# All eight experts over half of the tokens at a time in the first sequence, in tiles of two unit chunks

## The chip, the cores and the metric

The kernel runs on one core of one Trainium2 chip. The core has five engines with an instruction stream each: TensorE (PE in the profile, its weight loads as PEld), VectorE (DVE), ScalarE (ACT), GpSimd (POOL) and SyncE (SP), whose queue issues the kernel's DMAs. Every engine takes its own instructions in order and waits on semaphores for the others. The metric is the device time of one execution in microseconds. Before the change it was 1373.06 us, the median of three runs (1371.94 to 1373.44).

## What is computed

Eight independent sequences of 512 tokens with 128 features go through four layers, each with a layer norm ahead of it and a residual sum behind: a selective scan ("mamba"), a mixture of eight experts, a windowed attention with 16 heads, and the same mixture of experts again. All is float32. The mixture of experts is where most products are:

```python
router_probs = softmax(x @ w_router)             # (tokens, 8)
gate_weights = softmax(x @ w_gating / 0.1)
g = einsum('bsh,ehf->ebsf', x, w_gate)           # 8 experts, 128 -> 512 units
u = einsum('bsh,ehf->ebsf', x, w_up)
h = silu(g) * u
expert_out = einsum('ebsf,efh->ebsh', h, w_down) # 512 units -> 128
cw = router_probs * gate_weights
cw = cw / (sum(cw, axis=-1, keepdims=True) + 1e-09)
out = einsum('ebsh,bse->bsh', expert_out, cw)
```

Every token goes through all eight experts.

## The kernel before, in words

**The experts.** Tokens lie on the free axis (up to 512 of them, one bank of PSUM), features or units on the 128 partitions. The 512 units of an expert are four chunks of 128 (`NFC`). For each chunk TensorE makes g and u, and a little later adds the chunk's part to y, the expert's output. Each of these is three matmuls (`matmul3`), since every float32 operand is held as the sum of two rounded parts, "hi" and "lo": hi x hi, lo x hi, hi x lo.

Between u and y lies what this text calls the h pipeline (`hidden`, lines 1180 to 1212): ScalarE takes silu of g from the bank, VectorE multiplies it with u, ScalarE or VectorE rounds h to its hi part ("CAST h<-h"), and POOL (or VectorE) subtracts to get lo. While ScalarE holds the tables of an exponential set early in the kernel, silu is made in a second form: tanh on ScalarE and one VectorE instruction more (`halved`). When the four chunks of y are there, VectorE multiplies y with the expert's weights for the tokens, which SP has spread over the partitions from a small tensor in DRAM (`cwb`, lines 1138 to 1155), and POOL adds it to `acc` (`weighted`, lines 1114 to 1136). For the first expert VectorE writes `acc` itself.

**The stream.** All of this is one stream over two mixture layers (k), eight sequences (b), the passes of a sequence (`passes`, lines 1106 to 1112) and the four chunks. For all sequences but the very first a pass is one expert over all 512 tokens. In the first sequence the experts 0 to 3 (`SPLIT = 4`) go over the first 256 tokens, then over the second 256, and then experts 4 to 7 over all 512:

```python
parts = [(e, slice(c * HALF, c * HALF + HALF)) for c in range(2) for e in range(SPLIT)]
return parts + [(e, whole) for e in range(SPLIT, NE)]
```

The scan of sequence 0 is itself made in two halves of tokens, so its first half goes into the experts before its second half is done.

**The order.** A planner written in Python (`Clock`, `Lanes`) decides at build time in which order instructions stand on each engine. The stream of g, u and y is its main line on TensorE; beside it run "lanes" that it puts in where their inputs are due by its own cost figures: the h pipelines, the scans of the following sequences, the layer norms and routing (`ffn_prep`), the attention, and at the start the loading of the expert weights (`ffn_weights`). The eight banks are shared out by it: experts may hold six (`MOST`), a new y a seventh; the others may hold four. A tile of g or u takes one bank, whatever its width, from its first product until ScalarE (g) or VectorE (u) has read it.

**The weights.** The 24 weight matrices of 256 KB are loaded once by SP into a few stage tiles. ScalarE rounds each to hi ("CAST wu<-stageu") and POOL or VectorE subtracts to get lo; then its stage tile is free for the load three places on. Those of the experts from 5 on (`EARLY`) are rounded only after the first half of sequence 0 has been prepared.

**The scan of a following sequence** (`mamba_front`, `mamba_back`) needs on ScalarE two silus, two tanhs, then after a table load an exponential and a logarithm over `mdelta` and four exponentials `mdec`; on TensorE the transposition tp_m, the product mh, the products mde and mbc, eight spreads (mbx and mcc, one 512-wide product each) and the output product mo; on VectorE the convolution, four scans and a dozen products. Its result goes to DRAM (`x_1`), is loaded again (`x_f`), normed, and transposed (tp_f) into the next sequence's `xt_f`.

Since operations are recorded by one helper, nearly all instructions show its line, L264, and are told apart by their tiles.

Of the kernel before, what the change touches and what calls it, by code (L numbers as in the profile page):

```python
# [108 lines left out]
PREP_DUE = 0.8  # L109
ATT_LEAD = 2.5  # L110
EARLY = 5
SPLIT = 4
EARLIEST = 2 * (DEPTH + 1)


# [257 lines left out]
def block_kernel(ctx: ExitStack, tc: tile.TileContext, x, pack_a, pack_b, pack_c, w_qkv, mask, mask_t, w_o,  # L373
# [110 lines left out]
    def matmul3(dst, w, v, start=True, stop=True, after=0.0):  # L484

        clock.beside = False
        pe.matmul(dst, w[0], v[0], start=start, stop=False, after=after)
        pe.matmul(dst, w[1], v[0], start=False, stop=False)
        return pe.matmul(dst, w[0], v[1], start=False, stop=stop)
# [609 lines left out]
    def ffn_stream():  # L1099

        pending = []
        spread = []
        state = {}
        ends = {}

        def passes(k, b):

            whole = slice(0, L)
            if k or b:
                return [(e, whole) for e in range(NE)]  # L1110
            parts = [(e, slice(c * HALF, c * HALF + HALF)) for c in range(2) for e in range(SPLIT)]
            return parts + [(e, whole) for e in range(SPLIT, NE)]

        def weighted(k, b, e, cs, y, there):

            key = k, b, e, cs.start
            if ("cwb", key) not in state:
                yield lambda: ("cwb", key) in state
            cwb, come = state.pop(("cwb", key))
            yield "V", max(there, come)  # L1120
            left = state.setdefault(("left", k, b), [len(passes(k, b))])
            if e == 0:
# [12 lines left out]
            if left[0] == 0:  # L1135
                lanes.add(ffn_finish(k, b, state.pop(("acc", k, b))), rank=FRANK, ready=t)

        def spreads():

            for k in range(2):  # L1140
                for b in range(B):
                    todo = passes(k, b)
                    for i, (e, cs) in enumerate(todo):
                        at = k * B + b + (i * NFC + NFC - 1) / (len(todo) * NFC)
                        yield lambda: ("cw", k, b) in done and done["cw", k, b][2] >= cs.stop
                        yield lambda: pos[0] >= at and len(spread) < 2
                        cwd, there, _ = done["cw", k, b]
                        yield "S", there
                        spread.append(e)
                        n = cs.stop - cs.start  # L1150
                        cwb = fp.tile([P, L], F32, tag="cwb", name=f"cwb{k}_{b}_{e}_{cs.start}", bufs=2)[:, :n]
                        state["cwb", (k, b, e, cs.start)] = cwb, sp.dma_start(
                            out=cwb.rearrange("p (t q) -> p t q", q=P),
                            in_=cwd[None, cs.start // P : cs.stop // P, e, :].to_broadcast([P, n // P, P]),
                        )

        def can(f, hs, sure=0.0):

            return len(hs) > 2 and clock.there(hs[2] + sure) and (f > 0 or bank("experts", MOST + 1))

        def downs():

            while len(pending) > SHALLOW:
                f, hs = pending[0][4:]
                if len(pending) < DEPTH and not can(f, hs, SURE):
                    break
                while not can(f, hs):
                    yield True
                down(*pending.pop(0))

        def down(k, b, e, cs, f, hs):
            if f == 0:
                state["y"], = take("experts", [[P, L]], [f"y{k}_{b}_{e}"])
            y = state["y"][:, : cs.stop - cs.start]
            w = [t[:, f * P : (f + 1) * P] for t in wgt["d", e]]
            t = matmul3(y, w, hs, start=(f == 0), stop=(f == NFC - 1))
            if f == NFC - 1:
                lanes.hurry(weighted(k, b, e, cs, y, t))

        def hidden(i, g, there, us, hs, nm):  # L1180

            if i > 2:
                yield lambda: ends.pop(("lo", i - 3), None)
            yield "A", there
            n = size(g)
            h = fp.tile([P, L], F32, tag="h", name=f"h{nm}", bufs=3)[:, :n]

            halved = clock.table == 0 and clock.now < clock.hold
            if halved:
                act.activation(h, g, AF.Tanh, scale=0.5)  # L1190
                yield "V"
                s = dve.scalar_tensor_tensor(h, h, 1.0, g, ALU.add, ALU.mult)
            else:
                s = act.activation(h, g, AF.Silu)
# [12 lines left out]
            (dve.tensor_copy if v + HI_BIAS < a else act.copy)(hs[0], h)  # L1207
            yield "PV"
            ends["lo", i] = quicker(n, V_BIAS).tensor_tensor(hs[1], h, hs[0].bitcast(F32), ALU.subtract)
            hs.append(ends["lo", i])  # L1210

        lanes.hurry(spreads())
        i = 0
        for k in range(2):
            for b in range(B):
                todo = passes(k, b)
                for n, (e, cs) in enumerate(todo):
                    while (k, b) not in ready or ready[k, b][1] < cs.stop:
                        yield True
                    xt = [t[:, cs] for t in ready[k, b][0]]  # L1220
                    if n == len(todo) - 1:
                        ready.pop((k, b))
                    while ("d", e) not in done:
                        yield True
                    for f in range(NFC):
                        nm = f"{k}_{b}_{e}_{cs.start}_{f}"
                        fs = slice(f * P, (f + 1) * P)
                        pos[0] = k * B + b + (n * NFC + f) / (len(todo) * NFC)
                        while not bank("experts", MOST):
                            yield True  # L1230
                        g = take("experts", [[P, L]], [f"g{nm}"])[0][:, : cs.stop - cs.start]
                        t = matmul3(g, [t[:, fs] for t in wgt["g", e]], xt)
                        us = []
                        hs = [
                            fp.tile([P, L], F32R, tag=f"h{j}", name=f"h{j}{nm}", bufs=DEPTH + 1)[:, : size(g)]
                            for j in range(2)
                        ]
                        lanes.hurry(hidden(i, g, t, us, hs, nm))
                        yield
                        while not bank("experts", MOST):  # L1240
                            yield True
                        u = take("experts", [[P, L]], [f"u{nm}"])[0][:, : size(g)]
                        us += u, matmul3(u, [t[:, fs] for t in wgt["u", e]], xt)
                        yield
                        yield from downs()
                        pending.append((k, b, e, cs, f, hs))
                        i += 1
                        yield
        while pending:
# [528 lines left out]
```

## Time and profile before

| | before |
|---|---|
| median of three runs | 1373.06 us |
| the profiled execution's own time | 1372.12 us |
| its span, first to last instruction | 1370.3 us |
| mean granted TensorE clock | 0.994 |
| TensorE busy | 1334.7 us, 97% |
| VectorE busy | 1040.2 us, 76% |
| ScalarE busy | 966.5 us, 71% |
| POOL busy | 931.4 us, 68% |
| TensorE's first g of sequence 0 | at 41.12 us |
| first 512-wide g (expert 4) | at 106.53 us |
| the output product mo of sequence 1's scan | at 99.72 us |

Times in the trace count from the first instruction. A row of the order of time has the start, the length, the engine, the line, the operation with its output and inputs, the shape and the number of equal instructions. The ends of matmuls are modelled, so the distance between the starts of rows that follow each other is a better measure of what a matmul costs than its length. A row of waits has the waiting engine and tile, the releasing engine and tile, the sum in us, the number of waits and the longest. A row of stages has the stage, its length, for each engine its busy time and (x) instructions, then the clock granted to TensorE as a share of full speed, the share of DMA and GB/s.

### The profile page before, as it was taken

What the parts mean: (1) busy time and instruction counts of PE and PEld (TensorE: products, weight loads), DVE (VectorE), ACT (ScalarE), POOL (GpSimd) and SP (SyncE); (2) the same over time, 40 slices, a digit from 0 to 9 for tenths busy, and PEclk for the clock granted to TensorE, in tenths of its full rate; (3) what the DMA queues carried; (4) which work ended last, traced back from release to release, by engine and by line L of the source; (5) the groups of instructions that cost most, each with busy time, mean ns of one, the idle gap of its engine ahead of it and who ended that gap; (6) DMA issues with size and microseconds to landing.
All of it is one profiled execution on the core that took longest, in us unless ns stands there. A gap on an engine that the chain in (4) does not pass through costs nothing. (4 is left out here: it accounts for less than half of the span.)

```text
span 1370.3 us, 29702 instructions
## 1 busy us (share of the span) xinstructions
PE 1334.7 (97%) x10328; PEld 1053.5 (77%) x10328; DVE 1040.2 (76%) x3132; ACT 966.5 (71%) x1701; POOL 931.4 (68%) x1050
## 2 busy tenths in 40 slices
PE   7789999999999999999999999999999999999997
PEld 6667777777878877777777777777777777778886
DVE  6886888788888556898878887888878878754443
ACT  7478587786785556776777787877777768775654
POOL 4576676666767577676766757767576676677776
PEclk9999999999999999999999999999999999999999
DMA  3221222233221431335435455453454443232111
GB/s 125 74 68 50 64 46 75 65 86 86 54 60 35 70 77 46 77 71 121 98 88 111 87 117 111 93 107 86 106 116 90 113 91 74 65 71 54 40 39 39
DMA packets 230846, 107.77 MB, mean 79 GB/s; under 512 B 86401, under 2 KB 226600, under 8 KB 230696
## 3 DMA queue, kind: packets, MB, share of 16 engines
q1 hardware_dynamic: 230696, 105.87, 34.2%
q8 instruction: 82, 1.34, 0.4%
q14 instruction: 68, 0.56, 0.1%
HBM read 77.64 MB, written 27.79 MB: 77 GB/s over the span
## 5 line engine op out<-in xcount | busy, mean ns | idle before, releaser
L264 POOL TENSOR_TENSOR h<-h,h 128x512 fp32r<-128x512 f32 (+1 forms) x508 | 641.9, 1272 | 299.4 <-ACT h L264 236.3
L264 PE MATMUL u<-xt_f,wu 128*128 128x512 f32 (+1 forms) x1584 | 454.7, 395 | 7.5 <-ACT h L264 6.1
L264 PE MATMUL g<-xt_f,wg 128*128 128x512 f32 (+1 forms) x1584 | 452.5, 394 | 3.4 <-DVE cwb L264 1.0
L264 PE MATMUL y<-h,wd 128*128 128x512 f32 (+1 forms) x1584 | 449.9, 393 | 5.0 <-POOL h L264 2.8
L264 ACT CAST h<-h 128x512 fp32r<-128x512 f32 (+1 forms) x467 | 279.5, 604 | 200.4 <-DVE h L264 198.7
L264 DVE TENSOR_TENSOR h<-u,h 128x512 f32<-128x512 f32 (+1 forms) x424 | 283.0, 673 | 168.9 <-PE u L264 104.4
L264 ACT ACTIVATE h<-g 128x512 f32<-128x512 f32 (+1 forms) x528 | 305.0, 583 | 113.9 <-PE g L264 85.6
L264 PEld LDWEIGHTS u<-xt_f,wu 128*128 128x128 f32 x1584 | 288.4, 189 | 78.1 <-ACT h L264 9.8
L264 PEld LDWEIGHTS y<-h,wd 128*128 128x128 f32 x1584 | 289.9, 188 | 75.2 <-POOL h L264 3.9
L264 PEld LDWEIGHTS g<-xt_f,wg 128*128 128x128 f32 x1584 | 289.7, 189 | 72.8 <-DVE cwb L264 2.1
L264 POOL TENSOR_TENSOR acc<-acc,cwb 128x512 f32<-128x512 f32 (+1 forms) x115 | 146.7, 1275 | 52.4 <-DVE cwb L264 31.3
L264 ACT ACT_TABLE_LOAD x110 | 141.1, 1283 | 26.0 <-PE g L264 24.3
L264 DVE CUSTOM_DVE_ANT_0 amasked<-as,maskq 128x60 f32<-128x60 f32 x640 | 95.3, 213 | 4.0 <-PE as L264 3.5
L264 DVE TENSOR_TENSOR cwb<-y,cwb 128x512 f32<-128x512 f32 (+1 forms) x115 | 77.2, 671 | 19.2 <-PE y L264 10.8
L264 DVE TENSOR_TENSOR apt<-aw,maskk 125x400 f32<-125x400 f32 (+2 forms) x160 | 87.0, 572 | 0.1
L264 DVE SCALAR_TENSOR_TENSOR h<-h,g 128x512 f32<-128x512 f32 (+1 forms) x104 | 67.2, 649 | 23.4 <-ACT h L264 22.4
L264 ACT ACTIVATE apt<-apt 125x400 f32<-125x400 f32 (+2 forms) x160 | 81.8, 541 | 0.4
L264 DVE SCALAR_TENSOR_TENSOR h<-u,h 128x512 f32<-128x512 f32 (+1 forms) x104 | 67.6, 652 | 3.1
L264 DVE DVE_READ_ACCUMULATOR2_ANT amx<- 128x1 f32 x640 | 52.2, 82 | 0.0
L264 PEld LDWEIGHTS ao<-apt,v 125*32 125x32 f32 (+2 forms) x1280 | 27.4, 110 | 14.6 <-issue 4.7
L264 DVE CAST h<-h 128x512 fp32r<-128x512 f32 (+1 forms) x61 | 37.8, 624 | 1.0
L264 DVE COPY v<-avr 125x128 f32<-125x128 f32 (+2 forms) x40 | 21.1, 529 | 21.7 <-PE ao L264 18.0
(195 smaller groups left out, 1232.0 us busy)
## 6 DMA issues: line engine op xcount, KB each, us to landing
cwb<-cwd_f SPq DMA_DIRECT2D x124, 256.0 KB
aqd<-apc SPq DMA_DIRECT2D x32, 192.0 KB
ks<-aqd SPq DMA_DIRECT2D x48, 93.8 KB
x_fo<-x SPq DMA_DIRECT2D x16, 256.0 KB
aqd<-apc SPq DMA_DIRECT2D x32, 128.0 KB
x_f<-x SPq DMA_DIRECT2D x15, 256.0 KB
qs<-aqd SPq DMA_DIRECT2D x48, 75.0 KB
aod<-aos SPq DMA_DIRECT2D x24, 100.0 KB
```

Source lines behind the costliest of these rows:

```text
L264: f(*args, **kw)
```

## The change

In sequence 0 all eight experts go over the first 256 tokens, and then all eight over the second 256 (`SPLIT = 8`). A tile of g, u or h is again 512 wide, but holds two chunks of units for 256 tokens beside each other: columns 0 to 255 are chunk f, columns 256 to 511 chunk f+1. `products` fills a bank of g or u with two sets of three matmuls of 256 columns; the h pipeline works over the 512 columns at once; `down` adds the two halves of h to the same 256 columns of y with two sets of three matmuls. `chunks` gives the column ranges: two for a pass over 256 tokens, one for a pass over 512. All later sequences have one chunk to a tile as before. The planner is the same, and makes its order anew.

```diff
-SPLIT = 4
+SPLIT = 8
...
+        def chunks(cs):
+
+            n = cs.stop - cs.start
+            return [slice(c, c + n) for c in range(0, L, n)]
...
             y = state["y"][:, : cs.stop - cs.start]
-            w = [t[:, f * P : (f + 1) * P] for t in wgt["d", e]]
-            t = matmul3(y, w, hs, start=(f == 0), stop=(f == NFC - 1))
-            if f == NFC - 1:
+            for cols in chunks(cs):
+                w = [t[:, f * P : (f + 1) * P] for t in wgt["d", e]]
+                t = matmul3(y, w, [h[:, cols] for h in hs[:2]], start=(f == 0), stop=(f == NFC - 1))
+                f += 1
+            if f == NFC:
                 lanes.hurry(weighted(k, b, e, cs, y, t))
...
-            n = size(g)
-            h = fp.tile([P, L], F32, tag="h", name=f"h{nm}", bufs=3)[:, :n]
+            n = L
+            h = fp.tile([P, L], F32, tag="h", name=f"h{nm}", bufs=3)
...
-                    for f in range(NFC):
+                    n_chunks = len(chunks(cs))
+                    for f in range(0, NFC, n_chunks):
                         nm = f"{k}_{b}_{e}_{cs.start}_{f}"
-                        fs = slice(f * P, (f + 1) * P)
-                        pos[0] = k * B + b + (n * NFC + f) / (len(todo) * NFC)
+                        pos[0] = k * B + b + (n * NFC + f + n_chunks - 1) / (len(todo) * NFC)
+                        def products(dst, w):
+                            for c, cols in enumerate(chunks(cs)):
+                                fs = slice((f + c) * P, (f + c + 1) * P)
+                                t = matmul3(dst[:, cols], [t[:, fs] for t in wgt[w, e]], xt)
+                            return t
...
-                        g = take("experts", [[P, L]], [f"g{nm}"])[0][:, : cs.stop - cs.start]
-                        t = matmul3(g, [t[:, fs] for t in wgt["g", e]], xt)
+                        g = take("experts", [[P, L]], [f"g{nm}"])[0]
+                        t = products(g, "g")
...
-                        u = take("experts", [[P, L]], [f"u{nm}"])[0][:, : size(g)]
-                        us += u, matmul3(u, [t[:, fs] for t in wgt["u", e]], xt)
+                        u = take("experts", [[P, L]], [f"u{nm}"])[0]
+                        us += u, products(u, "u")
```

More of the change, by code (lines that the diff above doesn't have):

```diff
@@ L1224, in ffn_stream @@
                         yield True
[L1225 removed]
+                    n_chunks = len(chunks(cs))
+                    for f in range(0, NFC, n_chunks):
                         nm = f"{k}_{b}_{e}_{cs.start}_{f}"
[L1227 to L1228 removed]
+                        pos[0] = k * B + b + (n * NFC + f + n_chunks - 1) / (len(todo) * NFC)
[4 more added lines that the diff above has]
+                            return t
                         while not bank("experts", MOST):
                             yield True
[L1231 to L1232 removed]
+                        g = take("experts", [[P, L]], [f"g{nm}"])[0]
+                        t = products(g, "g")
                         us = []
                         hs = [
[L1235 to L1236 removed]
+                            fp.tile([P, L], F32R, tag=f"h{j}", name=f"h{j}{nm}", bufs=DEPTH + 1) for j in range(2)
                         ]
```

## The prediction

> **What bounds the kernel now.** First the page's busy table: TensorE is busy for 97% of the span and no other engine above 76%, so time can be won only where TensorE is not streaming. The slices show that all of this lies in the first 100 us and in the last 10.
>
> ```profile
> PE 1334.7 (97%) x10328; PEld 1053.5 (77%) x10328; DVE 1040.2 (76%) x3132; ACT 966.5 (71%) x1701; POOL 931.4 (68%) x1050
> ...
> PE   7789999999999999999999999999999999999997
> ```
>
> Next the busy time by stages. From 75 to 95 us TensorE works less than VectorE, and part of it at a granted clock of one half; from 100 us on it is full. From 107 to 500 us the stages leave about 4.4 us of it unused in all, after 500 next to nothing until the tail.
>
> ```profile
> 75.00:80.00 5.00, 1.95 (x16) 1.69 (x14) 4.13 (x9) 4.92 (x8) 1.99 (x3) 1.00 0.61 161
> 80.00:85.00 5.00, 3.02 (x12) 2.65 (x13) 4.44 (x16) 4.97 (x12) 3.81 (x11) 0.50 0.00 0
> 85.00:90.00 5.00, 4.01 (x22) 3.31 (x22) 5.00 (x9) 2.69 (x8) 4.72 (x5) 0.82 0.19 56
> 90.00:95.00 5.00, 4.28 (x31) 3.57 (x30) 4.97 (x11) 2.83 (x8) 3.57 (x5) 1.00 0.26 76
> 100.00:150.00 50.00, 49.95 (x260) 40.19 (x260) 37.56 (x82) 36.88 (x67) 35.30 (x41) 1.00 0.17 45
> ```
>
> Third, TensorE's waits between 41 us (its first g) and 107 us, the stage that the change rewrites. They sum to 11.2 us; the largest is a single one of 5.0.
>
> ```profile
> PE u L264 <- ACT h L264: 5.9, 2, 5.0
> PE y L264 <- POOL h L264: 2.1, 3, 1.1
> PE u L264 <- DVE mv L264: 0.9, 1, 0.9
> PE y L264 <- DVE h L264: 0.7, 1, 0.7
> ```
>
> Last, the order of time. ScalarE goes into sequence 1's scan with two table loads and six passes over delta, and does no silu between 73.79 and 81.54. TensorE fills the banks that the experts may hold with 256-wide tiles of 0.36 us each and stands from 76.95 to 81.98.
>
> ```profile
> 74.62 1.28 ACT L555 ACT_TABLE_LOAD   x1
> 75.91 1.30 ACT L264 ACTIVATE mdelta<-mdelta 128x512 f32<-128x512 f32 x2
> ...
> 80.25 1.28 ACT L264 ACT_TABLE_LOAD   x1
> ```
>
> ```profile
> 76.43 0.52 PE L264 MATMUL g<-xt_f,wg 128*128 128x256 f32 x3
> 81.98 1.01 PE L264 MATMUL u<-xt_f,wu 128*128 128x256 f32 x3 [5.03 <-ACT h L264]
> ...
> 95.53 0.53 PE L264 MATMUL y<-h,wd 128*128 128x256 f32 x3
> 95.89 0.52 PE L264 MATMUL g<-xt_f,wg 128*128 128x256 f32 x3
> ```
>
> The last two rows give my unit: three 256-wide products take 0.36 us from start to start. Three of 512 take 0.70 (119.11 to 119.81).
>
> **The change part by part.** *TensorE's products.* Experts 4 to 7 go from 48 sets of three 512-wide products (4 experts, 4 chunks, g, u and y) to 96 sets of 256: 96 x 0.36 - 48 x 0.70 = +0.96 us, all on the path.
>
> [...]
>
> *The h pipeline.* Experts 0 to 3 ran as 32 tiles of 256, now 16 of 512; means of a row are silu 384 ns against 596, cast 404 against 618, VectorE's product 417 against 686, POOL's subtraction 745 against 1308. Saved over the sequence: ScalarE 16 x (0.17 + 0.19) = 5.8 us, VectorE 16 x 0.15 = 2.4, POOL 16 x 0.18 = 2.9. Given back: the tanh form of silu (one VectorE instruction more) now covers 8 tiles of 512 instead of 12 of 256, 8 x 0.68 - 12 x 0.41 = +0.5 on VectorE. Closing y goes from 8 halves and 4 wholes to 16 halves: VectorE 16 x 0.41 - 8 x 0.41 - 4 x 0.69 = +0.5, POOL 14 x 0.756 - 6 x 0.756 - 4 x 1.304 = +0.8, and 16 spreads of 128 KB on SP's queue for 8 of 128 and 4 of 256. None of these engines is the bound as a sum, so none of this is a gain by itself. What counts is how much TensorE can do beside sequence 1's scan.
>
> *TensorE's cover.* A bank now holds 0.72 us of products, not 0.36. In the built order there stand after sequence 1's first spread (mbx, at 74.18 before) and ahead of the point where the banks are full: g and u of expert 5, y of 4, g and u of 6, each 0.72, and two more spreads of 0.24 (96.97 to 97.21), 4.1 us. Before, there were six sets of 0.36 and one spread, 2.4 us. The stall of 5.0 shrinks by these 1.7 us, to about 3.
>
> *How far TensorE is at a common point.* That point is the output product of sequence 1's scan ("mo"), at 99.72 us before: from there TensorE of before streams without waits. Counting units ahead of it in the two built orders gives 81 before (28 of g, 28 of u, 25 of y) and 106 after (38, 38 and 30). Left of sequence 0 (192 units): before 15 x 0.36 + 48 x 0.70 = 39.0 us; after 86 x 0.36 = 31.0. That is 8.0 us less, of which 0.4 goes back for one transposition (tp of sequence 2) that now comes later: **-7.6 us** if mo comes at the same time. The +0.96 is in it.
>
> *When mo comes.* The chain to it goes over VectorE. Ahead of mo's addition VectorE had 41 h instructions of 256 at a spacing of 0.335 (66.83, 67.17, 67.50), 13.7 us, and has 28 of 512 at 0.60, 16.8 us: it is asked for more because TensorE is further on. With one more y and one more weight remainder, and three small ones fewer, +3.7 us. This is the upper bound: nothing of it absorbed. VectorE is idle for 10 us of 41 to 101, though (60 less the 50.0 busy), much of it waiting for ScalarE's and TensorE's next piece, of which there are half as many now. The lower bound is -1: the scan's steps come earlier where VectorE waited. From 83 to 101 it is 98% busy and absorbs nothing; the h work that falls there is 3.7 us before (11 x 0.335) and 4.8 after (8 x 0.60). I take **+1.0 us**, that difference, nearest to the saturated rows.
>
> *Weights and DMA order.* Expert 7's u weights are ready at 88.35 before (end of POOL's third subtraction from 84.60 on) and were not wanted until after 120; now TensorE comes to them at about 89. Loads wait for a stage tile and pass cwb spreads on SP, two more of them ahead of the last load than before; wg and wu of expert 7 were issued at 74.91 and 76.84, so their data is there and the casts behind the scan block set the time. Cost 0 taken, bounds 0 and +3 (the cast behind two silus and one subtraction of 1.27 more on POOL). What hides it is the scan block itself, ahead of which TensorE has no use for them; if they are late nothing covers it, since TensorE takes its products in order.
>
> *Sequence 1's entry.* Its transposition came 22.2 us after mo (99.72 to 121.90). Now 62 units and 2.8 us of others stand between, 25.1 us, while its load on SP's queue is issued later: it stands behind the spread for expert 2's second half, whose buffer comes free with expert 0's second y, 14 units after mo, 1.8 + 5.0 + 0.9 = 7.7 us against 5.0 before (99.72 to 104.74). Covered by little; 0 taken, up to +2.
>
> *The rest.* From the fifth expert of sequence 5 (about 505 us) on, the orders of all engines are the same, and what TensorE does is full in both. Between 107 and 505 they differ; TensorE lost 4.4 us there, and could lose nothing or twice as much: bounds -4.4 and +4.4, 0 taken, since nothing in the two orders speaks for either. The tail keeps its order.
>
> Sum: -7.6 + 1.0 = -6.6 on the profiled execution's 1372.12 us (span 1370.3), 1365.5. That execution lies 0.94 below the median of the runs shown, so in their terms **1366.5 us**, 0.5% faster. About 0.2%, 2.7 us, is what a measurement of this kernel can tell from no change.
>
> **The rivals.**
> *The clock stays up and the chain is not delayed.* At 40 to 45 us the granted clock was 0.50 after a wait of only 2.35 us (38.20 to 40.55), and 0.50 again after the 5.0; after single waits of 1.1 it stayed 1.00. A stall of 3 lies between; I take the halving, which costs some 2.5 us (81.98 to 87 at half).
> [...]
> Without it, and with mo 1 us early: -7.6 - 1 - 2.5 = -11.1, 1362. Against it: VectorE, not TensorE, brings mo.
>
> *VectorE takes the gain.* Nothing of the 3.7 us is absorbed and the stage to 505 loses 2 more: -7.6 + 3.7 + 2 = -1.9, 1371. For it: 5.00 and 4.97 busy of 5 from 85 to 95. Against: ten idle microseconds before.
>
> *Slower: the weights come too late.* Eight experts are wanted in half of the tokens' time. TensorE stands at g or u of expert 7 until POOL has split it, and everything behind waits. Every microsecond after about 89 costs one; slower by 0.2% needs 6.6 + 2.7 = 9.3, so u of expert 7 ready after 98. At 100 it would be 1373.06 - 6.6 + 11 = 1377. For it: three subtractions in a row on POOL and casts behind the scan block. Against: both loads were issued 12 us ahead.
>
> **How the numbers follow.** Forecast 0.60 (within 1363 to 1370); clock and chain 0.10; VectorE takes it 0.20, of which 0.08 under 1370.3; weights 0.10. Faster by over 0.2%: 0.60 + 0.10 + 0.08 = 0.78; within: 0.12; slower: 0.10. The range leaves out the slower case and half of the best: 1361.5 to 1372.5.
>
> **What the profile after would show.** The longest wait of TensorE near 77 to 83 us about 3 us, not 5; waits from 41 to 107 of some 6 to 8 us; mo at 100 to 102; g, u, y in sets of six at 0.72; sequence 1's first g about 6 us earlier than before; the same waits as before after 505 us. Wrong if mo comes after 105, if u of expert 7 waits for POOL, or if TensorE waits for sequence 1's xt_f.

## The result, and the profile after

The changed kernel is slower: 1376.96 us median (1375.33 to 1380.33, 11 runs) against 1373.06 (1368.93 to 1375.45, 11 runs) beside it, a ratio of 1.0035 with a 95% interval of 1.0024 to 1.0046. Forecast were 1366.5 us and a range of 1361.5 to 1372.5; both the sign and the range were missed. Ratios in this text compare fast executions; one of the order with MAMBA_DUE at 1.05 below (1953 us, at a mean clock of 0.61) was slow and is left out. The profiled execution took 1377.14 us with a span of 1375.4, 5.1 more than before's.

The page's busy table and slices of the kernel after. TensorE is busy for 2.5 us more, and by slices (34.4 us each) the one from 138 to 172 us has fallen from 9 to 8; behind it nothing stands out.

```profile
PE 1337.2 (97%) x10472; PEld 1063.0 (77%) x10472; DVE 1040.0 (76%) x3113; ACT 960.6 (70%) x1668; POOL 930.0 (68%) x1038
...
PE   7889899999999999999999999999999999999998
```

Busy time by stages of the kernel after (stage, length, busy time and instructions of TensorE, weight loads, VectorE, ScalarE and POOL, then the clock). From 75 to 80 TensorE is now full where it was 1.95 of 5: the cover that the prediction counted is there. But it falls short from 80 to 95 (before: from 75 to 95), and VectorE is full from 85 on.

```profile
75.00:80.00 5.00, 5.00 (x41) 4.87 (x40) 4.45 (x10) 4.88 (x8) 4.79 (x5) 1.00 0.45 131
80.00:85.00 5.00, 1.80 (x12) 1.53 (x11) 4.41 (x11) 4.94 (x9) 3.05 (x8) 0.89 0.42 132
85.00:90.00 5.00, 3.58 (x20) 3.29 (x18) 5.00 (x8) 2.03 (x4) 4.07 (x3) 0.77 0.17 52
90.00:95.00 5.00, 3.95 (x21) 3.92 (x22) 5.00 (x10) 2.83 (x5) 3.19 (x4) 0.66 0.02 5
140.00:152.00 12.00, 10.71 (x54) 8.17 (x53) 10.38 (x19) 11.29 (x17) 5.62 (x6) 1.00 0.33 83
152.00:168.00 16.00, 13.02 (x45) 9.53 (x44) 13.13 (x20) 4.36 (x8) 4.56 (x4) 0.79 0.11 30
```

TensorE's waits of 41 to 107 us in the kernel after. Their sum is 11.5 us, but the 2.35 of the row lps_f were waited ahead of the first g (at 41.71; the kernel before waited the same 2.35 at 40.55, outside its stage). From the first g on it is 9.2 us, against 11.1 before (11.2 by the prediction's rounded rows), and not the 6 to 8 that were written down. The stall of 5.0 has become two, of 3.2 and 2.5, and the second is a new kind: on the routing of the second half of sequence 0.

```profile
PE mbx L264 <- ACT h L264: 3.2, 1, 3.2
PE cps_f L264 <- POOL cw_f L264: 2.5, 1, 2.5
PE lps_f L264 <- DVE xt_f L264: 2.4, 1, 2.4
PE g L264 <- DVE mv L264: 1.1, 1, 1.1
```

The order of time around them, kernel after. The row of waits names POOL, but POOL's product for cw_f had waited 1.72 us for s_f, a reciprocal of 0.15 us on VectorE. That stood in VectorE's order behind a scan of 1.20, a clip and a product of sequence 1's scan, and ran at 90.56, though its input (POOL's s_f) had been there since 83.72.

```profile
84.45 0.79 PE L264 MATMUL mbx<-mbc,sel 128*128 128x512 f32 x1 [3.20 <-ACT h L264]
...
88.45 1.20 DVE L264 TENSOR_TENSOR_SCAN mst<-mdec,mbx 128x512 f32<-128x512 f32 x1
89.58 0.46 DVE L264 TENSOR_SCALAR mdelta<-mdelta,cap 128x512 f32<-128x512 f32 x1
89.95 0.69 DVE L264 TENSOR_TENSOR mcc<-mcc,mst 128x512 f32<-128x512 f32 x1
90.56 0.15 DVE L264 RECIPROCAL s_f<-s_f 128x2 f32<-128x2 f32 x1
...
90.78 0.21 POOL L264 TENSOR_TENSOR cw_f<-cw_f,s_f 128x16 f32<-128x16 f32 x1 [1.72 <-DVE s_f L264]
91.05 0.38 PE L264 MATMUL cps_f<-ident,cw_f 128*16 128x128 f32 x1 [2.47 <-POOL cw_f L264]
```

Where the time went, by common points. The product mo of sequence 1's scan came 62.1 us behind the first g (before: 58.6), with 106 units done (before: 81). By the prediction's prices the changed kernel was then still 4.1 us ahead. Sequence 1's first g came at 138.96 instead of 143.95, 5.0 us earlier, though some of sequence 2's scan that TensorE had done by then before was still to come. From the product yp that closes sequence 5 (560.01 before, 565.53 after, 1192 units in both) on, the two run in step, some 5 us apart. So 8 to 9 us by the prediction's prices were lost between 104 and 565 us, where the prediction took 0.

Most of it is lost at sequence 2's scan. The same two stages of the kernel before, beside the last two rows of after above: TensorE is 1.29 us fuller in the first and 1.75 in the second, and the clock is 1.00, not 0.79.

```profile
140.00:152.00 12.00, 12.00 (x55) 9.71 (x54) 11.47 (x18) 5.72 (x10) 6.38 (x5) 1.00 0.30 80
152.00:168.00 16.00, 14.77 (x72) 11.28 (x70) 12.77 (x20) 8.36 (x15) 9.34 (x7) 1.00 0.24 56
```

The order of time there, kernel after. VectorE's scan of 1.21 us ends at 156.69, and only behind it come the products h<-u that empty TensorE's banks. ScalarE had waited 3.34 us for the first of them, TensorE 0.92 and then 1.80; the g at 159.96 runs at half clock (three products of 512 in 1.65 instead of 0.86).

```profile
155.48 1.21 DVE L264 TENSOR_TENSOR_SCAN mst<-mdec,mbx 128x512 f32<-128x512 f32 x1
156.61 0.66 DVE L264 TENSOR_TENSOR h<-u,h 128x512 f32<-128x512 f32 x1
...
156.74 0.97 PE L264 MATMUL u<-xt_f,wu 128*128 128x512 f32 x3 [0.92 <-DVE mst L264]
...
157.31 0.62 ACT L264 CAST h<-h 128x512 fp32r<-128x512 f32 x1 [3.34 <-DVE h L264]
...
159.96 1.65 PE L264 MATMUL g<-xt_f,wg 128*128 128x512 f32 x3 [1.80 <-ACT h L264]
```

In the built orders, counted in units (a set of three 512-wide products is two), sequence 2's scan begins (its transposition tp_m) after 64 units before and 150 after, and its mo comes after 214 and 252: it is pressed into 102 units instead of 150.

### The profile page after: what moved, and what is told of

It reads as the page before. It is cut to its first block, busy times and chain, and to the rows that moved or that the text cites. A ratio compares the mean times of both kernels' runs of the same rounds, so it can differ in the third digit from the quotient of the medians.

```text
span 1375.4 us, 29918 instructions
## 1 busy us (share of the span) xinstructions
PE 1337.2 (97%) x10472; PEld 1063.0 (77%) x10472; DVE 1040.0 (76%) x3113; ACT 960.6 (70%) x1668; POOL 930.0 (68%) x1038
## 5 line engine op out<-in xcount | busy, mean ns | idle before, releaser
L264 POOL TENSOR_TENSOR h<-h,h 128x512 fp32r<-128x512 f32 x492 | 638.7, 1307 | 296.4 <-ACT h L264 255.5
L264 ACT CAST h<-h 128x512 fp32r<-128x512 f32 x455 | 278.8, 618 | 197.5 <-DVE h L264 195.7
L264 DVE TENSOR_TENSOR h<-u,h 128x512 f32<-128x512 f32 x412 | 280.5, 686 | 176.0 <-PE u L264 116.5
L264 ACT ACTIVATE h<-g 128x512 f32<-128x512 f32 x512 | 302.9, 596 | 122.5 <-PE g L264 83.1
L264 PEld LDWEIGHTS g<-xt_f,wg 128*128 128x128 f32 x1632 | 293.1, 190 | 72.4 <-ACT h L264 3.9
L264 DVE TENSOR_TENSOR cwb<-y,cwb 128x512 f32<-128x512 f32 (+1 forms) x119 | 77.9, 655 | 15.2 <-PE y L264 11.2
L264 DVE SCALAR_TENSOR_TENSOR h<-h,g 128x512 f32<-128x512 f32 x100 | 67.9, 681 | 20.4 <-ACT h L264 19.4
L264 DVE SCALAR_TENSOR_TENSOR h<-u,h 128x512 f32<-128x512 f32 x100 | 68.3, 684 | 3.1
L264 DVE CAST h<-h 128x512 fp32r<-128x512 f32 x57 | 36.6, 646 | 1.0
L264 PE MATMUL ao<-apt,v 125*32 125x100 f32 (+2 forms) x1280 | 36.4, 254 | 0.0
```

The costliest lines, as they stand in the source:

```text
L264: f(*args, **kw)
```

## The experiments

Two theories were set up. *Late scan*: sequence 2's scan is made later and faster than before, and stalls TensorE. *VectorE*: in-order VectorE has too much to do wherever a scan stands, and what TensorE waits for queues behind scan instructions; it delays mo of sequence 1 too. A plain rival to both is that every new order of this planner costs or saves some tenths of a per cent. In the texts written ahead of the runs, D is *late scan* and V is *VectorE*; A puts the loss on ScalarE's block of table loads and exponentials, S and P on the one or the other half of the change, and L (later 'no rule') is the plain rival.

**The two halves of the change.** First eight experts per half with one chunk to a tile (the kernel before with SPLIT = 8), then tiles of two chunks with four experts per half (the kernel after with SPLIT = 4).

```diff
-SPLIT = 4
+SPLIT = 8
```

> The kernel before with SPLIT = 8 alone: all eight experts over half of the tokens, tiles of one chunk, 256 wide. Its built order keeps the transposition that opens sequence 2's scan (tp_m) at 64 units, where the kernel before has it (the changed kernel: 150). Theory D (the loss comes from sequence 2's scan being put late, then crammed, which stalls TensorE from 149 to 169 us and halves its clock): no such stall, the time within 2 us of before, 1371 to 1375. Rival S (taking all eight experts by halves costs by itself, whatever the tiles): slower like the changed kernel, 1376 to 1378. Rival P (the pairing of chunks costs): as before, 1373.

1381.9 us, ratio 1.0052 (1.0038 to 1.0066). Sequence 2's scan began early (64 units, spread over 139), and TensorE stalled there all the same. Its waits of 107 to 175 us:

```profile
PE u L264 <- ACT h L264: 4.7, 3, 3.3
```

ScalarE, in the same kernel, had a table load, four passes and another load between its silus:

```profile
133.17 1.28 ACT L555 ACT_TABLE_LOAD   x1
134.47 1.95 ACT L264 ACTIVATE mdec<-mdelta,nega 128x512 f32<-128x512 f32 x3
136.45 0.72 ACT L264 ACTIVATE mdelta<-mdelta,nega 128x512 f32<-128x512 f32 x1
137.19 1.28 ACT L264 ACT_TABLE_LOAD   x1
```

So an early start alone doesn't prevent the stall.

```diff
-SPLIT = 8
+SPLIT = 4
```

> The changed kernel with SPLIT = 4: only experts 0 to 3 by halves, but in tiles of two chunks. Its built order opens sequence 2's scan at 148 units, as late as the changed kernel. Theory D: slower like the changed kernel, 1375 to 1379, with TensorE waits of 3 us or more and a halved clock between 140 and 175 us. Rival S: as before, 1373. Rival P: like the changed kernel, 1377, but with its waits spread over 41 to 105 us.

1380.83 us, ratio 1.0053 (1.0034 to 1.0072); sequence 2's scan from 148 units over 98, waits of 3.5 and 3.1 us already at 66 and 71 us. Either half of the change alone was no better than both together; neither of the two can be named the loser.

**The order alone.** The same products and tiles as the changed kernel, with a planner constant moved by a thirtieth. The planner also decides anew which engine rounds a tile of h, and which tiles take the tanh form; so the orders below are not the same instructions on every engine. VectorE rounds 57 tiles of h in the changed kernel, 61 in this order, and 59 to 75 in the others of the changed kernel.

```diff
-PRESS = 0.3
+PRESS = 0.31
```

> The changed kernel with one constant of the planner moved by 0.01 us (PRESS 0.30 to 0.31). The computation and the tiles are those of the changed kernel; the order made anew opens sequence 2's scan at 78 units, not 150, and mo of sequence 1 stands at 100 units, not 106. Theory D: the stall at 149 to 169 us is gone and the time comes down by 4 to 8 us, to 1368 to 1372, faster than before. Rivals S and P: 1376 to 1378, no change against the changed kernel. Theory L (any order moves the time by some us and no single place carries it): anywhere from 1368 to 1380, with the waits elsewhere.

1373.77 us, ratio 0.9993 (0.9984 to 1.0003): 0.4% less than the changed kernel with the same tiles. Sequence 2's scan began at 78 units, was spread over 156, and no clock fell there. The stall on the routing was larger than ever (waits of 41 to 107 us, same kernel):

```profile
PE cps_f L264 <- POOL cw_f L264: 4.0, 1, 4.0
```

And the kernel before, with a lag of its planner 2 ns larger:

```diff
-TO_PE = 0.11
+TO_PE = 0.112
```

> The kernel before with one constant of the planner moved by 0.002 us (TO_PE 0.110 to 0.112). The tiles are those of before; the order made anew opens sequence 2's scan at 118 units, not 64, with mo of sequence 1 at 89 units, not 81. Theory D: slower than before by 2 to 5 us (1375 to 1378), with TensorE waits and a halved clock at sequence 2's scan. Rivals S and P: as before, 1373. Theory L: anywhere from 1368 to 1380.

1383.54 us, ratio 1.0067 (1.0052 to 1.0083); sequence 2's scan from 118 units over 118, waits of 2.03 and 1.66 us at 154 and 164. The products and tiles are those of before (VectorE rounds 81 tiles of h instead of 61), and the order costs twice what the change did. Of the ranges written ahead of these four runs none that names a place or a half of the change (D, S, P) held; L's, 1368 to 1380, held for PRESS 0.31 and not for this one. What stands is that the changed kernel's products and tiles, in another order, take 0.9993: its loss is one of order.

**VectorE relieved.** Four kernels keep their own order, but twelve VectorE instructions of a sequence's scan are planned and not issued: in sequence 1's scan, in sequence 2's, in all seven, and in all seven of the kernel before. The edit for sequence 1's; for the others the condition is b == 2, or always true:

```diff
+        less = dict(planned_only=b == 1)
...
-                bxs[i] = bx, dve.tensor_tensor(bx, bx, xb, ALU.mult)
+                bxs[i] = bx, dve.tensor_tensor(bx, bx, xb, ALU.mult, **less)
...
-                dve.scalar_tensor_tensor(bx, decs[i], 1.0, bx, ALU.subtract, ALU.mult)
+                dve.scalar_tensor_tensor(bx, decs[i], 1.0, bx, ALU.subtract, ALU.mult, **less)
...
-                decs["c", i] = dve.tensor_scalar(decs[i], decs[i], cap[:, i : i + 1], 1e-4, ALU.min, ALU.max)
+                decs["c", i] = dve.tensor_scalar(
+                    decs[i], decs[i], cap[:, i : i + 1], 1e-4, ALU.min, ALU.max, **less
+                )
```

> The changed kernel in its own order, with twelve VectorE instructions of sequence 1's scan left out (the four products of mbx with mxb, the four of mbx with the decay, and the four clips of mdec), so its result is not the reference's. They take some 9 us of VectorE between 77 and 98 us in the changed kernel's profile. Theory V (VectorE, in its own order, holds TensorE in the stage of sequence 1's scan: the scan's products, and the reciprocal of the routing that stands behind them): the wait of 2.5 us for POOL's cw is gone, and one of the two spells of halved clock; mo comes at most 59 us after the first g (62.1 now), the time falls by 3 to 7 us against the changed kernel, to a ratio of 0.998 to 1.001. Rival A (ScalarE's block of tables and exponentials holds it): mo stays at 61 to 62 us after the first g, the time falls by less than 1.5 us.

> The changed kernel in its own order, with the same twelve VectorE instructions left out of sequence 2's scan alone (not the reference's result). Theory V for the second stage: the waits from 149 to 169 us shrink from 4.6 us to under 2, the halved clock from 156 to 168 us is gone, and the time falls by 3 to 6 us against the changed kernel, to a ratio of 0.999 to 1.001. Rival A: the waits follow ScalarE's three table loads between 136 and 150 us and stay within 1 us of what they are, the time falls by less than 1.5 us.

> The changed kernel in its own order, with the twelve VectorE instructions left out of the scans of all sequences from 1 on (not the reference's result). To be read against the next run. Theory V: with VectorE relieved the gain that was forecast appears: 4 to 8 us faster than the kernel before with the same left out. Theory L (the order made for these tiles is simply worse, wherever VectorE stands): slower than it by 2 us or more, or the same.

> The kernel before in its own order, with the same left out of all scans from sequence 1 on (not the reference's result). Its waits were 11.4 us from 41 to 107 us and 4.4 us from 107 to 505. Theory V: it gains less than the changed kernel does, 2 to 6 us against before, since its largest stall (5.0 us at 77 to 82) waits for ScalarE. Theory L: it gains as much as the changed kernel.

The ratios to the kernel before are in the last column; the others are distances between common points in the profiled executions, in us.

| | first g to mo of seq. 1 | mo of 1 to mo of 2 | mo of 2 to mo of 7 | ratio (95%) |
|---|---|---|---|---|
| before | 58.60 | 57.70 | 285.49 | 1 |
| before, all relieved | 58.42 | 57.11 | 285.58 | 0.9990 (0.9978 to 1.0003) |
| after | 62.14 | 69.40 | 297.46 | 1.0035 (1.0024 to 1.0046) |
| after, seq. 1's relieved | 58.98 | 68.37 | 297.47 | 1.0008 (0.9992 to 1.0023) |
| after, seq. 2's relieved | 62.12 | 65.66 | 297.45 | 0.9997 (0.9981 to 1.0012) |
| after, all relieved | 58.80 | 64.56 | 294.83 | 0.9967 (0.9953 to 0.9980) |

The distances fall where the relieved scan stands: 3.2 us ahead of mo of sequence 1 (and 1.0 just behind it), 3.7 at sequence 2's, 2.6 in the later ones. The kernel before, relieved in the same way, gains 0.7 us in all, so it isn't merely that a scan with twelve instructions fewer is shorter. Behind mo of sequence 7 the profiled executions of the four relieved kernels lose 1.7 to 2.9 us again up to the yp that closes sequence 5, in the three of the changed kernel with one more spell of halved clock (501 to 515 us), so the ratios, from many executions, are the firmer reading: 3.7, 5.2 and 9.3 us less than the changed kernel, and 1.4 less than before (not clear of noise). Theory A, which allowed under 1.5 us, falls for the changed kernel. Theory V's ranges held for sequence 1's scan and for the ratio of sequence 2's. There the waits came down to 2.3 us, not under 2, and 3.4 us of halved clock were left of 6.8; the last two runs gained less than it had said.

This settles the largest part. Relieved on both sides, the change goes from 0.35% slower to 0.23% faster: some 8 us of the 12 that it lost (3.5 ahead of mo, 8.7 behind) it lost to these instructions on VectorE. What the other 4 are due to stays open. In the kernel after with sequence 1's scan relieved, the wait on the routing is nearly gone (waits of 41 to 107 us); the one ahead of sequence 1's spread mbx stays, at 3.0 instead of 3.2:

```profile
PE mbx L265 <- DVE mst L265: 3.0, 1, 3.0
...
PE cps_f L265 <- POOL cw_f L265: 0.4, 1, 0.4
```

With both kernels relieved the change is worth 0.9967 against 0.9990, some 3 us in its favour. That is half of the forecast, and under the 4 to 8 us that theory V had said.

**Scans opened earlier.** If lateness were the matter, opening scans ahead of time would mend it.

```diff
-MAMBA_DUE = 1.0
+MAMBA_DUE = 1.4
```

> The changed kernel with the planner's margin for opening a scan (MAMBA_DUE) at 1.4 of a sequence instead of 1.0: sequence 2's scan begins (tp_m of sequence 2) 128 units into the stream instead of 150, its output product mo comes after 216 units instead of 252 (the kernel before has 64 and 214); sequence 1's scan and its mo (106 units) stay where they are. Theory 'late scan' (the loss after mo of sequence 1 comes from sequence 2's scan being pressed into too short a stretch): the waits of 107 to 175 us go from 4.6 to about 2 and the halved clock there goes; ratio to the kernel before 1.000 to 1.001. Theory 'VectorE has too much to do wherever the scan stands' : waits of 107 to 175 us still 4 or more, ratio 1.003 to 1.005. The first stage, 41 to 107 us, is as in the changed kernel by both: 11 to 12 us of waits, mo of sequence 1 62 us behind the first g.

```diff
-MAMBA_DUE = 1.0
+MAMBA_DUE = 1.6
```

> As the run before it, with the margin at 1.6: sequence 2's scan begins after 80 units, ahead of mo of sequence 1 (which then has 92 units ahead of it instead of 106), and its mo comes after 162. Theory 'late scan': no stall at sequence 2's scan (waits of 107 to 175 us under 2, clock 1.00), ratio 0.998 to 1.000 as in the run with PRESS at 0.31 (0.9993). Theory 'VectorE has too much to do': two scans then share VectorE with the h work from 85 us on; mo of sequence 1 is not earlier by the 14 units (5 us) that it lost, and waits appear on h or y between 100 and 140; ratio 1.002 to 1.006.

```diff
-MAMBA_DUE = 1.0
+MAMBA_DUE = 2.0
```

> As the two runs before it, with the margin at 2.0: sequence 2's scan begins after 78 units and its mo comes after 148, sequence 1's mo stays at 102 units. Theory 'late scan': as at 1.6, ratio 0.998 to 1.000. Theory 'VectorE has too much to do': mo of sequence 1 more than 62 us behind the first g, stalls from 100 to 150; ratio 1.002 to 1.006.

Ratios of 1.0071 (1.0057 to 1.0084), 1.0095 (1.0080 to 1.0110) and 1.0166 (1.0151 to 1.0182). *Late scan* falls, as far as lateness goes: the earlier the scans, the slower the kernel. (These scans are also pressed into fewer units, 88, 82 and 70; that comes back below.) With 1.4 the waits of 107 to 175 us did go down, from 4.6 to 3.1, but those of 175 to 300 went up from 2.7 to 6.5. The VectorE theory had said 4 or more for the first of them, the right direction, and a range that the first two reach past (1.003 to 1.005 and 1.002 to 1.006 against 1.0071 and 1.0095); the third, 1.0166, lies far outside it. Two stages, 107 to 175 and 175 to 300 us, of the kernel before, and then of the one with 2.0:

```profile
107.00:175.00 68.00, 66.72 (x313) 51.35 (x312) 52.61 (x108) 47.15 (x81) 43.36 (x44) 1.00 0.21 54
175.00:300.00 125.00, 124.27 (x589) 97.72 (x588) 106.36 (x207) 99.37 (x166) 88.84 (x94) 1.00 0.26 65
```

```profile
107.00:175.00 68.00, 57.88 (x386) 48.72 (x385) 51.34 (x105) 41.52 (x70) 32.05 (x39) 0.95 0.16 46
175.00:300.00 125.00, 119.16 (x555) 90.63 (x554) 92.81 (x187) 86.60 (x148) 82.02 (x88) 1.00 0.29 69
```

TensorE misses 8.8 us in the first of them. VectorE isn't fuller over the whole stage (51.34 against 52.61); it is full in pieces: from 117 to 127, in the middle of sequence 2's scan, VectorE is busy for 10.00 us of 10 and TensorE for 6.08.

**How far a scan is spread.** These runs suggested another reading: what counts is over how many units of TensorE's stream sequence 2's scan is spread. It had been read off after the runs, so four new orders of the changed kernel were to test it.

```diff
-PRESS = 0.3
+PRESS = 0.4
```

> The changed kernel with the planner's PRESS at 0.40 instead of 0.30, the same instructions in another order: sequence 2's scan is spread over 144 units (from 80 to 224), sequence 3's over 210; mo of sequence 1 has 94 units ahead of it. Theory 'spread' (a scan pressed into fewer units than about 150 asks more of VectorE and ScalarE in that stretch than they have, and TensorE waits for h): ratio to the kernel before 0.998 to 1.001, waits of 107 to 300 us under 4, no halved clock from 107 us on. Theory 'start' (what counts is that sequence 2's scan begins before mo of sequence 1): the same, 0.998 to 1.001. Theory 'no rule' (each order is a draw): anything from 0.999 to 1.007.

```diff
-PRESS = 0.3
+PRESS = 0.25
```

> As the run before it, with PRESS at 0.25: sequence 2's scan is spread over 136 units (from 100 to 236), sequence 3's over 212; mo of sequence 1 at 106 units as in the changed kernel. Theory 'spread': 0.999 to 1.001, clearly under the changed kernel's 1.0035. Theory 'start': it begins at 100, between the 80 and the 150; 1.000 to 1.003. Theory 'no rule': anything from 0.999 to 1.007.

```diff
-TO_PE = 0.11
+TO_PE = 0.10
```

> The changed kernel with the planner's lag to TensorE (TO_PE) at 0.10 us instead of 0.11: sequence 2's scan begins at 150 units and is spread over 90 (after: 102), sequence 3's over 206 (after: 134). Theory 'spread': what scan 2 loses is as in the changed kernel or a little more, what scan 3 loses is gone: 1.002 to 1.004. Theory 'start': as the changed kernel, 1.0035. Theory 'no rule': anything from 0.999 to 1.007.

```diff
-MAMBA_DUE = 1.0
+MAMBA_DUE = 1.05
```

> The changed kernel with MAMBA_DUE at 1.05 instead of 1.0: sequence 2's scan begins at 150 units as in the changed kernel and is spread over 80 (after: 102), sequence 3's over 146 (after: 134). Theory 'spread': 1.004 to 1.007, slower than the changed kernel. Theory 'start': 1.0035. Theory 'no rule': anything from 0.999 to 1.007.

1.0048 (1.0035 to 1.0060), 1.0030 (1.0018 to 1.0041), 1.0032 (1.0022 to 1.0043) and 1.0073 (1.0060 to 1.0087). The theory of the spread has one hit, one just outside, and two misses on the slow side. The wide range of 'no rule' held three of the four. *Start*, that sequence 2's scan must begin ahead of mo, fared worse: the earliest start gave 1.0048, and the two that begin at 150 differ by 0.4%. The first miss came largely from the stage ahead of mo, through another door. TensorE waited for the weights of u, the prediction's slower rival, in an order in which the cast came late (TensorE's order of time, PRESS 0.4):

```profile
88.49 0.38 PE L264 MATMUL u<-xt_f,wu 128*128 128x256 f32 x1 [3.64 <-ACT wu L264]
89.84 1.44 PE L264 MATMUL u<-xt_f,wu 128*128 128x256 f32 x5 [0.97 <-POOL wu L264]
```

So the stage ahead of mo and the one behind it have to be kept apart. Three more orders, with nearly the same first stage (102 to 104 units ahead of mo), did that, and the loss behind mo was now named as the measure:

```diff
-SECOND = 0.1
+SECOND = 0.15
```

> The changed kernel with the planner's lag of a second step (SECOND) at 0.15 instead of 0.10, the same instructions in another order: mo of sequence 1 has 104 units ahead of it (changed kernel: 106), sequence 2's scan is spread over 150 (from 80 to 230; changed kernel 102), sequence 3's over 196. Theory 'spread': what is lost behind mo of sequence 1 against the kernel before (time from there to the yp at 1192 units, less 0.35 us for each unit) is 0 to 4 us, not 8.7; ratio 0.998 to 1.001. Rival 'no rule': lost 5 to 9 us as in most orders, ratio 1.002 to 1.005.

```diff
-SAME = 0.125
+SAME = 0.14
```

> As the run before it, with the planner's figure for a step on the same engine (SAME) at 0.14 us instead of 0.125: mo of sequence 1 after 104 units, sequence 2's scan spread over 150 (from 78 to 228), sequence 3's over 200. Theory 'spread': 0 to 4 us lost behind mo, ratio 0.998 to 1.001. Rival 'no rule': lost 5 to 9 us, ratio 1.002 to 1.005.

```diff
-SAME = 0.125
+SAME = 0.1
```

> The same constant at 0.10 us, to the other side: mo of sequence 1 after 102 units, sequence 2's scan spread over 102 (from 154 to 256), sequence 3's over 128, both as in the changed kernel. Theory 'spread': 7 to 11 us lost behind mo, ratio 1.003 to 1.006. Rival 'no rule': anything from 0.999 to 1.007.

0.9973 (0.9961 to 0.9985), 1.0005 (0.9994 to 1.0015) and 1.0096 (1.0075 to 1.0116). The table puts all orders beside each other. "Lost behind mo" is the time from mo of sequence 1 to the yp that closes sequence 5, less the 460.29 us of before, with 0.35 us added for each unit done ahead of mo beyond 81, and with 0.01 for each further 256-wide unit left and 0.4 for a tp_m left taken off. (In two orders yp stands 4 and 8 units early; 0.35 us is added for each.)

| order | units ahead of mo of 1 | seq. 2's scan: begins, spread over (units) | lost behind mo, us | ratio |
|---|---|---|---|---|
| after, PRESS 0.31 | 100 | 78, 156 | 0.8 | 0.9993 |
| before | 81 | 64, 150 | 0 | 1 |
| after, SECOND 0.15 | 104 | 80, 150 | 3.3 | 0.9973 |
| after, SAME 0.14 | 104 | 78, 150 | 5.1 | 1.0005 |
| after, PRESS 0.4 | 94 | 80, 144 | 5.3 | 1.0048 |
| before, SPLIT 8 | 81 | 64, 139 | 7.4 | 1.0052 |
| after, PRESS 0.25 | 106 | 100, 136 | 6.2 | 1.0030 |
| before, TO_PE 0.112 | 89 | 118, 118 | 7.8 | 1.0067 |
| after | 106 | 150, 102 | 8.7 | 1.0035 |
| after, SAME 0.1 | 102 | 154, 102 | 13.2 | 1.0096 |
| after, SPLIT 4 | 100 | 148, 98 | 7.5 | 1.0053 |
| after, TO_PE 0.10 | 106 | 150, 90 | 8.4 | 1.0032 |
| after, MAMBA_DUE 1.4 | 106 | 128, 88 | 15.6 | 1.0071 |
| after, MAMBA_DUE 1.6 | 92 | 80, 82 | 13.0 | 1.0095 |
| after, MAMBA_DUE 1.05 | 106 | 150, 80 | 13.8 | 1.0073 |
| after, MAMBA_DUE 2.0 | 102 | 78, 70 | 23.7 | 1.0166 |

The loss goes with the spread (rank correlation -0.93 over the sixteen orders, -0.95 over the seven made after the theory). The start of the scan orders it less: +0.56 over the sixteen, with 78 and 80 at both ends. In the seven fresh orders the two go together (starts of 78 to 100 with spreads of 136 to 150, of 150 to 154 with 80 to 102), so it is the two orders with MAMBA_DUE at 1.6 and 2.0, from which the theory had been read off, that part them. The number of tiles of h that VectorE rounds doesn't order the loss: 61 in the first row and in the last. In the three fresh orders the rank came out as written ahead, the sizes only in part: 3.3 lay within 0 to 4; 5.1 lay above it, with a ratio within the range; 13.2 lay above 7 to 11, and its ratio above 1.003 to 1.006. The rival's ranges for the ratio missed all three, its 5 to 9 us were met once (5.1). The spread ranks orders; it doesn't price them. The two orders with 102 units (8.7 against 13.2) are level up to mo of sequence 2 and part at sequence 3's scan: from mo of 2 to mo of 3 the one takes 72.35 us for 170 units, the other 76.88 for 168, with spreads of 134 and 128. What makes that difference was not traced.

The order with SECOND 0.15 beats both kernels: a median of 1371.4 us against 1374.54 of before on the same chip, 0.27% less by the ratio. Its profile shows a part of that. Ahead of mo it is 3.8 us in front of before by the prices above, behind it loses 3.3; its span is 1369.8 against 1370.3 of before's profile, whose execution (1372.12) was 2.4 us faster than the median beside these runs. Its two stages from 107 us on, to be held against those of before shown above:

```profile
107.00:175.00 68.00, 64.87 (x422) 56.22 (x421) 51.51 (x108) 44.98 (x76) 42.64 (x46) 1.00 0.26 60
175.00:300.00 125.00, 123.28 (x581) 96.05 (x580) 106.99 (x207) 96.94 (x160) 86.57 (x93) 1.00 0.27 65
```

Since this is the best of twelve orders of the changed kernel, while before was run in two, it doesn't show that the change is better at equal care for the order.

## Why the prediction was wrong

*TensorE's products, +0.96.* Held. Six 256-wide products take 0.72 us from start to start after (111.12 to 111.84), two units of 0.36.

*TensorE's cover, a stall of about 3 instead of 5.0.* Held: 3.20 at 84.45.

*How far TensorE is at mo, -7.6.* The count of units held, 106 against 81.

*When mo comes, +1.0.* Mis-sized: 62.1 against 58.6 from the first g, +3.5, almost the upper bound of 3.7. The runs agree with the mechanism named for that bound, nothing absorbed by VectorE: relieved, mo came 3.2 us earlier. The prediction chose between its bounds by the stage in which VectorE was saturated before, 83 to 101, and took only the h work that falls there. But VectorE's idle time ahead of that stage was no reserve: of 41 to 107 us it was busy for 56.9 us (before: 53.3) and still idle for 9.1, while the work that mattered queued up in the full stretch from 85 on.

*The clock.* The prediction took a wait of 2.35 us (38.20 to 40.55) for enough to halve the clock. In that trace the clock fell at 39.01, 0.8 us into this wait and behind another of 0.89; how much idling is enough was not shown. The forecast's case, a halving after a stall of about 3, came true, and one more halving after the 2.47 that had not been foreseen. By stages the clock was 0.89, 0.77 and 0.66 from 80 to 95 us, where before had 0.50, 0.82 and 1.00.

*Waits of 6 to 8 us from 41 to 107.* Failed: 9.2 from the first g on. The 2.47 on the routing is what is missing. The prediction named the queue behind the scan on ScalarE and POOL, but not the small routing steps of the second half of sequence 0 that stand behind scan instructions on VectorE. In the kernel before the one long stand, of 5.0, was for a bank.

*Weights, 0.* Held in this order; no u waited for POOL. In the order with PRESS 0.4 u waited 3.6 us for ScalarE's cast and 1.0 for POOL's subtraction, so the cover was as thin as the rival said.

*Sequence 1's entry, 0.* Held: its transposition came 25.3 us after mo (129.49) without a wait; 25.1 had been worked out. Its first g was 5.0 us earlier than before, 5.9 by each kernel's own first g; "about 6" had been written.

*The rest, 0 with bounds of 4.4 to both sides.* This step failed most: 8.7 us lost. Counted otherwise, from 100 us in the kernel before and 107 in the one after up to 520 us, TensorE left 4.5 and 9.6 us unused, +5.2, and the spell of halved clock from 159 to 166 us costs about 3 more. The bound of 4.4 was made from what TensorE had lost before, as if an order could lose at most twice that, and it left the clock out. "Nothing in the two orders speaks for either" was wrong as well: sequence 2's scan in 102 units instead of 150 could be read from them. Why the planner pressed it so was not traced. One reading, not shown, is that when sequence 0 goes by faster, the same scans have less of TensorE's stream to stand beside; other orders of the same tiles spread it over 150 and more.

*The rivals.* "VectorE takes the gain" had the cause right and its price too low: 3.7 + 2 where 3.5 + 8.7 came. Together with -7.6 these make the +4.6 that the two profiles have from first g to the close of sequence 5 (518.89 and 523.48); that is bookkeeping and no second proof, since 8.7 was reckoned from the same points with the prediction's prices. Its chance for a slower kernel, 0.10, lay on the weights, which held; that the sign was slower came from this rival's cause. "The same waits after 505 us" held but for the entry to the attention, 1.6 us at 511.53, where before had 1.2 at 496.85.

## What to carry to other kernels

In a stream that runs at 97% of one engine beside others at 68 to 76%, work that is taken off the full engine's first stage has to be followed through the next ones: the side work can then stand in a shorter stretch, and its in-order engines fill up in pieces while their averages stay the same (here VectorE was busy for 8.00 us of the 8 from 152 to 160 where before had 7.67, and for 76% of the span in both). So count, in the built order, how many units of the main stream each block of side work is spread over, before and after. And where a planner makes the order, measure what a change of a few per cent in its constants does (here 3% and 5% gave 0.9993 and 1.0073, and larger ones 0.9973 to 1.0166, with the same products and tiles) before a few tenths of a per cent are put down to an edit.

## What the runs showed of the hardware

*The clock behind short waits in a row.* In the kernel after, waits of 0.94, 0.35, 0.92 and 1.80 us within 11 us (149.08 to 159.96) were followed by a granted clock of 0.50 from 160 to 164 and 0.77 to 168. Waits of 3.20 and 2.47 were followed by 0.59 (84 to 88) and 0.73 (92 to 96). In another order, the changed kernel with PRESS 0.25, waits of 1.60, 1.35 and 1.52 us between 143 and 155 left the clock at a mean of 1.00 from 107 to 175 us. The three falls in the kernel after came at 83.89, 90.71 and 158.98, inside the waits of 3.20, 2.47 and 1.80; in the 4 us ahead of each TensorE had been busy for 1.35, 1.87 and 2.26 us (by the modelled ends). In the kernel before it had been busy for 2.02 and 0.98 of the 4 us ahead of the falls at 39.01 and 79.97. What tells the waits that a fall follows from the others was not shown.

*The start varies.* The first g came between 40.5 and 43.6 us in the profiled executions; in the changed kernel and its three relieved forms, which have one order of TensorE up to there, at 42.05, 41.99, 43.37 and 40.76. Distances between two points of one execution are therefore the safer reading, and single spans differ by that much without any cause in the edit.
